# Products of q and k computed in two halves of TensorE's columns

## The chip, the cores and the metric

The kernel runs on one core of a Trainium2 chip. A core has TensorE (matrix products, PE in the profile, PEld for its weight loads), VectorE (DVE), ScalarE (ACT), GpSimd (POOL) and the queues of SyncE (SP), each with its own list of instructions. They work side by side and wait for each other by semaphores. The metric is the device time of one execution in microseconds, the median of several runs.

## The reference

The input is one image of 384 channels and 192 x 192 pixels. Layer 0 is attention over channels, layer 1 a product with binarized weights. Cut to what matters:

```python
x = x + attention(group_norm(x))            # layer 0
x = x + binary_conv(group_norm(x))          # layer 1

def attention(x):                           # 8 heads of 48 channels each
    qkv = einsum('bchw,oc->bohw', x, w_qkv) + b_qkv        # 384 -> 1152 channels
    qkv = max over 2x2 pixels               # 192x192 -> 96x96 = 9216 pixels
    qkv = depthwise 3x3 convolution(qkv)
    q, k, v = split(qkv, 3, axis=1)
    q, k = q / norm(q), k / norm(k)         # over the pixels
    attn = einsum('bhcn,bhdn->bhcd', q, k) * temperature   # 48 x 48 a head
    out = sum of four top-k softmaxes of attn, each @ v
    return w_proj @ upsample(gelu(out)) + b_proj
```

The change concerns `attn`: for each head, 48 x 48 sums over 9216 pixels. Only the products within a head are used.

## The kernel before

The image is worked through in 24 units of 8 rows, which after pooling are 4 rows of 96 pixels (3 in the first unit, 5 in the last, because of the 3x3 convolution). A first pass computes the statistics of the group norm, a second one q and k (six maps of 128 channels each), a third one v (three maps) and the attention's output; then come the projection and layer 1. Each map of a unit is computed in three blocks, each with three matmuls into one PSUM buffer (three buffers in all), and VectorE takes the maxima out of PSUM:

```python
        for r0, nr, c0, ncol in BLOCKS:                       # 3 blocks
            ps = pqkv.tile([P, 512], F32, name="qkv")
            for t in range(CT):                               # CT = 3
                nc.tensor.matmul(
                    ps,
                    wq[:, t, m * P : (m + 1) * P],
                    x4[:, t, r0 : r0 + nr, c0 : c0 + ncol],
                    start=(t == 0),
                    stop=(t == CT - 1),
                )
            nc.vector.tensor_reduce(pl[...], ps.rearrange(...), AX.XY, ALU.max)
        # ... ScalarE adds the bias, ScalarE and VectorE do the 3x3 taps
```

For the products, pixels must lie on the partitions. VectorE transposes q and k in blocks of 32 x 32, and DMAs put the blocks in place (`room<-blocks` in the profile). Then chunks of 128 pixels are multiplied: q is the stationary operand (the weights), k the moving one. The sums stay in PSUM over all units, in three buffers `gram`, one for every 128 channels of q. A tile of 128 channels touches three or four heads, so 144 or 192 channels of k; these start at a multiple of 32 (B = 32), which makes 160, 192 and 160 columns:

```python
HD = C // HEADS                                               # 48
HEAD0 = [t * P // HD for t in range(CT)]
HEAD1 = [((t + 1) * P - 1) // HD for t in range(CT)]
D0 = [h * HD for h in HEAD0]
DN = [(h1 - h0 + 1) * HD for h0, h1 in zip(HEAD0, HEAD1)]     # 144, 192, 144
B0 = [d // B for d in D0]
BN = [-(-(d + n) // B) - b for d, n, b in zip(D0, DN, B0)]    # 5, 6, 5 blocks of 32
# ...
        def products(u):

            n, nk, q, k = of_unit(u)                          # nk chunks of pixels
            for i in range(nk):
                L = min(P, n * WP - i * P)
                for t in range(CT):
                    ins = nc.tensor.matmul(
                        gram[t][:, : BN[t] * B],
                        q[:L, t, i],
                        k[:L, B0[t] : B0[t] + BN[t], i],
                        start=u == 0 and i == 0,
                        stop=u == NU - 1 and i == nk - 1,
                    )
                    if u == NU - 1:
                        tc.keep_in_program_order(ins)

        for u in range(NU):
            # ...
            for m in range(2 * CT):                           # six maps: q, then k
                acc = tp.tile([P, (PR + 1) * WP], F32, name="dw")[:, : n * WP]
                qkv_unit(pqkv, xt, u, m, padded_qk[m], [(acc, 0, n)], None if u or m else bias)
                transposed(u, *divmod(m, CT), acc)
                # ... sums of squares on ScalarE
                if u and m == CT - 1:
                    products(u - 1)
                if m % CT == CT - 1:
                    moved(u, m // CT)                         # the DMAs of the blocks

    def gathered():                                           # in the third pass

        products(NU - 1)
        for t in range(CT):
            at = D0[t] - B0[t] * B
            nc.vector.tensor_copy(gsb[:, t, : DN[t]], gram[t][:, at : at + DN[t]])
        last_products.close()
```

The products of a unit are thus issued in the middle of the next unit. 22 units have three full chunks; the first one has a last chunk of 32 pixels, the last unit has four chunks. A scheduler orders the instructions of each engine; `keep_in_program_order` pins an instruction relative to others that are pinned.

Two other places of the kernel are used for comparison. The product of attention and v already works in four groups of 32 rows of the array, with a quarter of the channels in each:

```python
            for t in range(CT):
                for p in range(NP):                           # NP = 4
                    rows = slice(p * Q, (p + 1) * Q)          # Q = 32
                    nc.tensor.matmul(
                        pss[p][:PAIR],                        # PAIR = 96
                        aT[rows, t, p * PAIR : (p + 1) * PAIR],
                        chunk[c][rows, t, cols],              # 512 columns
                        start=(t == 0), stop=(t == CT - 1),
                    )
```

And the bias of q, k and v is corrected once, with nine matmuls that have one moving column each:

```python
        for m in range(NM):                                   # NM = 9
            nc.tensor.matmul(ps[:, m : m + 1], wg[:, m * P : (m + 1) * P], shift, start=True, stop=True)
```

Of the kernel before, what the change touches and what calls it, by code (L numbers as in the profile page):

```python
# [20 lines left out]
P = 128  # L21
C = 384
CT = C // P
# [4 lines left out]
HD = C // HEADS  # L28
# [4 lines left out]
NU = H // UR  # L33
# [9 lines left out]
HALF = P // 2  # L43
B = 32
# [27 lines left out]
D0 = [h * HD for h in HEAD0]  # L72
DN = [(h1 - h0 + 1) * HD for h0, h1 in zip(HEAD0, HEAD1)]

B0 = [d // B for d in D0]
BN = [-(-(d + n) // B) - b for d, n, b in zip(D0, DN, B0)]
PAIR = 2 * HD
NP = C // PAIR
Q = P // NP
# [27 lines left out]
def pair_rows():  # L107
# [6 lines left out]
    for p in range(NP):  # L114
        v[p * Q : (p + 1) * Q] = p * PAIR + np.stack([i, HD + i, np.where(i < HD - Q, Q + i, 2 * Q + i)], 1)
    for t in range(CT):
        o[:PAIR, t] = t * PAIR + np.arange(PAIR)
        o[PAIR:, t] = CT * PAIR + t * Q + i
    assert sorted(v.flat) == sorted(o.flat) == list(range(C))
# [28 lines left out]
def conv_preact_kernel(ctx: ExitStack, tc: tile.TileContext, a: dict, out: bass.AP):  # L148
    nc = tc.nc
# [27 lines left out]
    def unit(u, pool=big, parts=1, pieces=1):  # L177
        xt = pool.tile([P, CT, UPX], F32, name="xt", tag="big")
        n = CT // parts
        for t in range(0, CT, n):  # L180

            for j in range(0, UPX, UPX // pieces if t == CT - 1 else UPX):
                px = slice(j, j + UPX // pieces if t == CT - 1 else UPX)
                nc.sync.dma_start(xt[:, t : t + n, px], xv[u][:, t : t + n, px])  # L184
        return xt
# [27 lines left out]
    def right(name, bufs=1, stack=att):  # L213
        return stack.enter_context(tc.tile_pool(name=name, bufs=bufs, side="right"))

    ap = right("att")
    ssq = ap.tile([P, 2 * CT, NU], F32, name="ssq")
    gsb = ap.tile([P, CT, max(DN)], F32, name="gsb")
    osum = ap.tile([P, CT, NAB], F32, name="osum")
    aT = right("aT").tile([P, CT, C], F32, name="aT")  # L220

# [34 lines left out]
    with tc.tile_pool(name="p1", bufs=1, side="right") as p1, tc.tile_pool(name="p1ps", bufs=2, space=PSUM) as psp:  # L256
# [17 lines left out]
        for i in range(NU):  # L274
            u = NU - 1 - i
# [7 lines left out]
            for t in range(CT):  # L283
                if t == (u + 1) % SHARE:
                    at = NB + i // SHARE
# [8 lines left out]
                b, k = divmod(seen[t], BATCH)  # L294
                seen[t] += 1
                for j in range(UPX // 512):
                    at = (k * (UPX // 512) + j) * 6
# [41 lines left out]
    def rows(u):  # L339

        return (1 if u else 2), (PR if u < NU - 1 else PR + 1)

    def qkv_unit(pqkv, xt, u, m, pl, parts, before=None):


        x4 = xt.rearrange("p t (r w) -> p t r w", w=W)
        lo, hi = rows(u)
        for r0, nr, c0, ncol in BLOCKS:
            ps = pqkv.tile([P, 512], F32, name="qkv")
            for t in range(CT):  # L350
                nc.tensor.matmul(  # L351
                    ps,
                    wq[:, t, m * P : (m + 1) * P],
                    x4[:, t, r0 : r0 + nr, c0 : c0 + ncol],
                    start=(t == 0),
                    stop=(t == CT - 1),
                )
            nc.vector.tensor_reduce(  # L358
                pl[:, 2 + r0 // 2 : 2 + (r0 + nr) // 2, 1 + c0 // 2 : 1 + (c0 + ncol) // 2],
                ps.rearrange("p (i a j b) -> p i j a b", a=2, b=2, j=ncol // 2),  # L360
                AX.XY,
                ALU.max,
            )
        if before:
            before(pqkv.tile([P, 512], F32, name="qkv")[:, :NM])
        new = pl[:, 2 : 2 + PR, 1 : 1 + WP]
        nc.scalar.activation(new, new, AF.Identity, bias=bq[:, m : m + 1])  # L367
        for acc, r0, n in parts:
            acc2 = acc.rearrange("p (r w) -> p r w", w=WP)
            for k in range(9):  # L370
                r = lo - 1 + r0 + k // 3
                src = pl[:, r : r + n, k % 3 : k % 3 + WP]
                if k == 0:
                    nc.scalar.activation(acc2, src, AF.Identity, bias=bdw[:, m : m + 1], scale=wdw[:, m, 0:1])  # L374
                else:
                    nc.vector.scalar_tensor_tensor(acc2, src, wdw[:, m, k : k + 1], acc2, ALU.mult, ALU.add)  # L376
        if u < NU - 1:
            nc.scalar.copy(pl[:, 0:2, :], pl[:, PR : PR + 2, :])  # L378
# [4 lines left out]
    with pairs, tc.tile_pool(name="p2t", bufs=2, side="right") as tp:  # L383
        gram = [pg.tile([P, 512], F32, name=f"gram{t}") for t in range(CT)]
        qkT = room[:, : 2 * size].rearrange("p (s n) -> p s n", s=2)

        def of_unit(u):

            lo, hi = rows(u)
            n = hi - lo + 1  # L390
            nk = -(-n * WP // P)
            q, k = qkT[:, 0, : nk * C], qkT[:, 1, : nk * C]
            return (
                n,
                nk,
                q.rearrange("p (t k c) -> p t k c", t=CT, k=nk),
                k.rearrange("p (b k c) -> p b k c", k=nk, c=B),
            )

        def transposed(u, s, t, acc):  # L400
            n, nk, *_ = of_unit(u)
            to = blocks[:, s, : nk * C].rearrange("p (j t k c) -> p t k j c", j=NBP, t=CT, c=B)[:, t]
            full, more = divmod(n * WP // B, NBP)
            nc.vector.transpose(to[:, :full], acc[:, : full * P].rearrange("p (k j c) -> p k j c", j=NBP, c=B))  # L404
            if more:
                src = acc[:, full * P : n * WP].rearrange("p (j c) -> p j c", c=B)
                nc.vector.transpose(to[:, full, :more], src)

        def moved(u, s):

            n, nk, q, k = of_unit(u)
            for j in range(NBP):
                src = blocks[:, s, j * nk * CT * B : (j + 1) * nk * CT * B]
                for i in range(NBP):
                    at, to = slice(i * B, (i + 1) * B), slice(j * B, (j + 1) * B)
                    if s == 0:
                        nc.sync.dma_start(
                            q[to].rearrange("p t k (i c) -> p i (t k) c", i=NBP)[:, i],
                            src[at].rearrange("p (m c) -> p m c", c=B),
                        )  # L420
                    else:
                        nc.sync.dma_start(  # L422
                            k[to].rearrange("p (t i) k c -> p i t (k c)", i=NBP)[:, i],
                            src[at].rearrange("p (t m) -> p t m", t=CT),
                        )

        def products(u):

            n, nk, q, k = of_unit(u)
            for i in range(nk):  # L430
                L = min(P, n * WP - i * P)
                for t in range(CT):
                    ins = nc.tensor.matmul(  # L433
                        gram[t][:, : BN[t] * B],
                        q[:L, t, i],
                        k[:L, B0[t] : B0[t] + BN[t], i],
                        start=u == 0 and i == 0,
                        stop=u == NU - 1 and i == nk - 1,
                    )
                    if u == NU - 1:  # L440
                        tc.keep_in_program_order(ins)

        for u in range(NU):

            for v in range(u, u + KEEP + 1):
                if v not in kept:
                    kept[v] = unit(v % NU)
            xt = kept.pop(u)
            lo, hi = rows(u)
            n = hi - lo + 1  # L450
            for m in range(2 * CT):
# [3 lines that stand above are left out]
                sq = tp.tile([P, (PR + 1) * WP], BF16, name="sq", bufs=1)  # L455
                nc.scalar.activation(sq[:, : n * WP], acc, AF.Square, accum_out=ssq[:, m, u : u + 1])  # L456
# [3 lines that stand above are left out]
                    moved(u, m // CT)  # L460

    def gathered():

        products(NU - 1)
        for t in range(CT):
            at = D0[t] - B0[t] * B
            nc.vector.tensor_copy(gsb[:, t, : DN[t]], gram[t][:, at : at + DN[t]])
        last_products.close()

    wpr = ctx.enter_context(tc.tile_pool(name="wpr", bufs=1)).tile([P, CT, C], F32, name="wpr")  # L470
# [130 lines left out]
    with ExitStack() as vs:  # L601
# [15 lines left out]
        def attention(g):  # L617
# [4 lines left out]
            for t in range(CT):  # L622
                for p in range(NP):
                    rows = slice(p * Q, (p + 1) * Q)
                    nc.tensor.matmul(  # L625
                        pss[p][:PAIR],
                        aT[rows, t, p * PAIR : (p + 1) * PAIR],
                        chunk[c][rows, t, cols],
# [8 lines left out]
        for u in range(NU):  # L637
# [9 lines left out]
            for m in range(CT):  # L647
                parts = []
                for c in range(first // CR, last // CR + 1):
                    r0, r1 = max(first, c * CR), min(last, c * CR + CR - 1)  # L650
# [262 lines left out]
```

## Time and profile before

| what | value |
|---|---|
| time, median of 3 runs (lowest, highest) | 2239.83 us (2238.95, 2241.53) |
| span of the profiled execution | 2237.0 us |
| TensorE clock granted | 1.0 throughout |
| first pass (statistics), until TensorE's q and k products begin | 0 to 150 us |
| second pass (q, k and their products) | 150 to 1349 us |
| third pass (v, softmax, attention) | 1311 to 1958 us |
| projection and layer 1 | 1958 to 2237 us |

In the profile, L351 are the products that make q, k and v (`qkv`), L433 the products of q and k (`gram`), L625 attention times v (`ops`), L336 the correction of the bias. A group's row gives the line, the engine, the operation, what is written and read, the number of records, then the busy time in us and the mean duration in ns, and last the idle time before them and what ended it. The chain that ended last is followed from the last instruction back to what released each step; its lengths add up to the span, so a share of it is a share of the time. In it, a row is a start, a length and the work of that stretch. A busy TensorE says little by itself, since matmuls are pipelined; the distance from one start to the next says how long one really takes.

### The profile page before, as it was taken

The numbers are of one execution on the slowest core, as the hardware profiler recorded it, in microseconds if no ns is written. First come the engines' busy times: TensorE is split into PE (matmuls) and PEld (weight loads), VectorE is DVE, ScalarE is ACT, GpSimd is POOL, SyncE is SP. The second block draws the span as 40 slices with busy tenths as digits, with TensorE's granted clock in tenths as the row PEclk, the third lists the DMA queues.
The fourth block names the chain that finished last, engine by engine and source line by source line (L and its number), as shares of the span: only waits on it lengthen the run. The fifth ranks groups of instructions, "written<-read, shape, count | busy, mean of one in ns | idle before, by whom it ended". The sixth has DMA issues, their size and how long they took to land.

```text
span 2237.0 us, 19501 instructions
## 1 busy us (share of the span) xinstructions
PE 2085.8 (93%) x6135; PEld 989.3 (44%) x6135; DVE 1902.5 (85%) x3267; ACT 819.6 (37%) x1419; POOL 210.8 (9%) x329
## 2 busy tenths in 40 slices
PE   0049999999999999999999999999999999999998
PEld 0024444444444444444444444443444444455555
DVE  5668888888888888888888898987787878899998
ACT  4542222222222222222222221225333232398876
POOL 1000000000000000000000000000000000077765
PEclk9999999999999999999999999999999999999999
DMA  9962222222222222222222312105221212379997
GB/s 398 418 274 64 64 68 70 75 95 70 69 64 68 70 74 95 70 69 64 68 70 72 98 30 105 53 11 211 85 85 43 87 67 101 127 277 407 424 425 328
DMA packets 209719, 302.66 MB, mean 135 GB/s; under 512 B 162224, under 2 KB 165072, under 8 KB 209616
## 3 DMA queue, kind: packets, MB, share of 16 engines
q1 hardware_dynamic: 199296, 248.18, 31.8%
q10 hardware_dynamic: 10320, 53.25, 5.8%
q8 instruction: 48, 0.79, 0.1%
q14 instruction: 55, 0.45, 0.1%
HBM read 216.04 MB, written 56.62 MB: 122 GB/s over the span
## 4 chain that ended last, share of the span: by engine, by line
PE 81%; DVE 10%; DMA 5%; ACT 1%; SPq 1%; issue 0%; DVEq 0%; ACTq 0%
PE qkv L351 64%; PE l1ps L792 6%; PE yps L580 6%; DVE chunk L376 5%; DMA xt<-in_x_dram 5%; PE gram L433 3%; DVE pooled L358 2%; PE ops L625 2%; DVE dw L376 1%; SPq L184 1%; DVE xt L592 1%; ACT chunk L374 0%; PE qkv L270 0%; ACT pooled L367 0%; SPq L422 0%
## 5 line engine op out<-in xcount | busy, mean ns | idle before, releaser
L351 PE MATMUL qkv<-xt,wq 128*128 128x512 f32 x3888 | 1679.2, 593 | 0.0
L351 PEld LDWEIGHTS qkv<-xt,wq 128*128 128x128 f32 x3888 | 735.1, 190 | 918.1 <-issue 821.9
L376 DVE SCALAR_TENSOR_TENSOR dw<-pooled,small,dw 128x384 f32<-128x384 f32 (+2 forms) x1152 | 708.7, 615 | 118.8 <-ACT dw L374 93.7
L358 DVE TENSOR_REDUCE pooled<-qkv 128x128 f32<-128x512 f32 x648 | 442.5, 684 | 67.1 <-PE qkv L351 66.8
L376 DVE SCALAR_TENSOR_TENSOR chunk<-pooled,small,chunk 128x384 f32<-128x384 f32 (+3 forms) x696 | 369.5, 545 | 70.9 <-ACT chunk L374 53.7
L378 ACT COPY pooled<-pooled 128x196 f32<-128x196 f32 x207 | 73.6, 356 | 761.5 <-DVE dw L376 542.8
L367 ACT ACTIVATE pooled<-pooled,small 128x384 f32<-128x384 f32 x216 | 133.0, 616 | 402.8 <-DVE pooled L358 389.4
L773 ACT ACTIVATE signs<-xt,nmean 64x1536 fp8e4<-64x1536 f32 x144 | 226.5, 1573 | 41.7 <-PE yps L580 26.0
L792 PE MATMUL l1ps<-signs,wb 128*128 128x384 fp8e4 x864 | 152.2, 326 | 0.0
L580 PE MATMUL yps<-chunk,wpr 128*128 128x384 f32 x396 | 138.2, 487 | 2.7 <-DVE xt L592 2.7
L270 PE MATMUL qkv<-wq,late 128*32 128x384 f32 x18 | 9.0, 665 | 140.3 <-ACT late L292 140.3
L801 DVE SCALAR_TENSOR_TENSOR xt<-l1ps,small,xt 128x768 f32<-128x768 f32 x144 | 138.3, 1007 | 0.0
L592 DVE SCALAR_TENSOR_TENSOR xt<-yps,small,xt 128x768 f32<-128x768 f32 x132 | 128.1, 1012 | 10.8 <-PE yps L580 4.4
L298 DVE BATCH_NORM_STATS2 room<-xt 128x6 f32<-128x512 f32 x144 | 88.1, 678 | 51.0 <-DMA xt<-in_x_dram 50.9
L609 POOL MEMSET pooled<- 128x196 f32 x3 | 0.8, 263 | 1300.6 <-DVE dw L376 1300.6
L456 ACT ACTIVATE sq<-dw 128x384 bf16<-128x384 f32 (+2 forms) x144 | 75.3, 523 | 112.4 <-DVE dw L376 112.4
L792 PEld LDWEIGHTS <-wb 128*128 128x128 fp8e4 x864 | 83.7, 97 | 72.3 <-issue 14.2
L374 ACT ACTIVATE dw<-pooled,small 128x384 f32<-128x384 f32 (+2 forms) x144 | 100.4, 697 | 2.2
L287 ACT ACTIVATE room<-xt 128x1536 bf16<-128x1536 f32 x48 | 71.2, 1483 | 66.4 <-DMA xt<-in_x_dram 65.7
L580 PEld LDWEIGHTS yps<-chunk,wpr 128*128 128x128 f32 x396 | 73.2, 190 | 44.3 <-issue 3.6
L404 DVE STREAM_TRANSPOSE blocks<-dw 128x384 f32<-128x384 f32 (+1 forms) x144 | 82.0, 569 | 3.4
L751 POOL COPY rest<-signs 9x384 int32<-9x384 int32 (+1 forms) x144 | 72.4, 503 | 64.5 <-ACT signs L773 59.0
(115 smaller groups left out, 622.1 us busy)
## 6 DMA issues: line engine op xcount, KB each, us to landing
xt<-in_x_dram SPq DMA_DIRECT2D x81, 2304.0 KB, 13.4
out_dram<-xt ACTq DMA_DIRECT2D x17, 2304.0 KB, 15.6
room<-blocks SPq DMA_DIRECT2D x736, 36.0 KB, 2.0
xt<-in_x_dram SPq DMA_DIRECT2D x26, 768.0 KB, 9.0
out_dram<-xt ACTq DMA_DIRECT2D x12, 768.0 KB, 8.7
out_dram<-xt SPq DMA_DIRECT2D x8, 768.0 KB, 3.4
wq<-in_w_qkvT_dram ACTq DMA_DIRECT2D x1, 1728.0 KB, 15.1
room<-blocks SPq DMA_DIRECT2D x32, 48.0 KB, 2.0
```

What stands on the lines that cost most here:

```text
L298: nc.vector.bn_stats(stats[b][:, t, at : at + 6], xt[:, t, j * 512 : (j + 1) * 512])
L351: nc.tensor.matmul(ps, wq[:, t, m * P : (m + 1) * P], x4[:, t, r0 : r0 + nr, c0 : c0 + ncol], start=(t == 0), stop=(t == CT - 1),)
L358: nc.vector.tensor_reduce(pl[:, 2 + r0 // 2 : 2 + (r0 + nr) // 2, 1 + c0 // 2 : 1 + (c0 + ncol) // 2], ps.rearrange("p (i a j b) -> p i j ...
L367: nc.scalar.activation(new, new, AF.Identity, bias=bq[:, m : m + 1])
L374: nc.scalar.activation(acc2, src, AF.Identity, bias=bdw[:, m : m + 1], scale=wdw[:, m, 0:1])
L376: nc.vector.scalar_tensor_tensor(acc2, src, wdw[:, m, k : k + 1], acc2, ALU.mult, ALU.add)
L404: nc.vector.transpose(to[:, :full], acc[:, : full * P].rearrange("p (k j c) -> p k j c", j=NBP, c=B))
L580: nc.tensor.matmul(ps, wpr[:, t, m * P : (m + 1) * P], o[:, t, :], start=(t == 0), stop=(t == CT - 1),)
L592: nc.vector.scalar_tensor_tensor(x5[:, m, r], yb, bpr[:, m : m + 1], x5[:, m, r], ALU.add, ALU.add)
L773: nc.scalar.activation(rows_of(sg, p, SAT[t] - HSHIFT[t][h]), xt[p, t, :].rearrange("p (r w) -> p r w", w=W), AF.Sign, bias=nmean1[p, t : ...
L792: nc.tensor.matmul(ps[:, j, : 2 * W], wb[:, t, m * P : (m + 1) * P], rows_of(sg, slice(0, P), SAT[t])[:, r0 + 2 * j : r0 + 2 * j + 2], sta ...
L801: nc.vector.scalar_tensor_tensor(blk, ps[:, :, : 2 * W], bl1[:, m : m + 1], blk, ALU.add, ALU.add)
```

## The change

The array of TensorE has 128 columns, one for each of the stationary operand's. [...] The change splits each tile of 128 channels of q into two halves. A half of 64 channels touches only two heads, so it needs only 96 channels of k (96 or 128 columns, since they begin at a multiple of 32), where the whole tile needed 160 or 192. The purpose is that fewer columns are multiplied for nothing, with two halves at work side by side.

`SIDES` has, for each of the six halves, the first channel of k and their number: (0, 96), (48, 96), (96, 96), (192, 96), (240, 96), (288, 96). All products are pinned, and so is the first matmul of the fourth map (m == CT): the products of a unit stand in one piece ahead of it, and the array is parted once a unit. What lies outside the two heads of a half isn't computed any more, so `gsb` is zeroed at the start, and the copies out of PSUM are six rather than three.

```diff
+SIDES = [(c // HD * HD, ((c + HALF - 1) // HD - c // HD + 1) * HD) for c in range(0, C, HALF)]
@@
     gsb = ap.tile([P, CT, max(DN)], F32, name="gsb")
+    nc.gpsimd.memset(gsb, 0.0)
@@ in qkv_unit
-                nc.tensor.matmul(
+                ins = nc.tensor.matmul(
                     ps,
                     ...
                 )
+                if m == CT and t == r0 == c0 == 0:
+
+                    tc.keep_in_program_order(ins)
@@ in products
-                for t in range(CT):
+                for j, (d, n) in enumerate(SIDES):
+                    t, p = divmod(j * HALF, P)
+                    b0, b1 = d // B, -(-(d + n) // B)
                     ins = nc.tensor.matmul(
-                        gram[t][:, : BN[t] * B],
-                        q[:L, t, i],
-                        k[:L, B0[t] : B0[t] + BN[t], i],
+                        gram[t][p : p + HALF, (b0 - B0[t]) * B : (b1 - B0[t]) * B],
+                        q[:L, t, i, p : p + HALF],
+                        k[:L, b0:b1, i],
                         start=u == 0 and i == 0,
                         stop=u == NU - 1 and i == nk - 1,
                     )
-                    if u == NU - 1:
-                        tc.keep_in_program_order(ins)
+
+                    tc.keep_in_program_order(ins)
@@ in gathered
-        for t in range(CT):
-            at = D0[t] - B0[t] * B
-            nc.vector.tensor_copy(gsb[:, t, : DN[t]], gram[t][:, at : at + DN[t]])
+        for j, (d, n) in enumerate(SIDES):
+            t, p = divmod(j * HALF, P)
+            at = d - B0[t] * B
+            nc.vector.tensor_copy(gsb[p : p + HALF, t, d - D0[t] : d - D0[t] + n], gram[t][p : p + HALF, at : at + n])
```

The built program shows two moves besides. The three matmuls that sum b_proj by groups (32 weight columns, one moving column), which stood after the last unit's products, now stand after the first one of unit 0's. And in each unit VectorE's pooling of the fourth map's first block stands some ten instructions later in its list.

## The prediction

> **What bounds the kernel now.** I read the page from the top (busy shares, then the chain that ended last), then the chain in order of time, then windows cut at one unit's edges, and last the waits of VectorE in that stage. The page:
>
> ```profile
> PE 2085.8 (93%) x6135; PEld 989.3 (44%) x6135; DVE 1902.5 (85%) x3267; ACT 819.6 (37%) x1419; POOL 210.8 (9%) x329
> ...
> PE qkv L351 64%; PE l1ps L792 6%; PE yps L580 6%; DVE chunk L376 5%; DMA xt<-in_x_dram 5%; PE gram L433 3%; DVE pooled L358 2%; PE ops L625 2%; DVE dw L376 1%; SPq L184 1%; DVE xt L592 1%; ACT chunk L374 0%; PE qkv L270 0%; ACT pooled L367 0%; SPq L422 0%
> ```
>
> TensorE sets the end, and the products that the change rewrites (`gram`, L433) lie on that path with 3% of the span. The change has no more than that to play with. Their group among the costliest:
>
> ```profile
> L433 PE MATMUL gram<-room 128*128 128x160 f32 (+3 forms) x438 | 67.6, 308 | 1.0 <-DMA room<-blocks 1.0
> ```
>
> 438 records are 219 matmuls: each fp32 matmul appears as two passes, each with its own weight load. The chain in order of time (start, length, what, how many records):
>
> ```profile
> 158.06 2.10 PE qkv L336 x18
> 160.15 62.85 PE qkv L351 x146
> 223.01 2.80 PE gram L433 x18
> 225.81 48.26 PE qkv L351 x112
> 274.07 2.60 PE gram L433 x18
> 276.68 46.35 PE qkv L351 x108
> 323.02 2.61 PE gram L433 x18
> ...
> 1349.50 3.71 PE gram L433 x24
> ...
> 1534.39 2.76 PE ops L625 x24
> 1537.16 7.92 PE qkv L351 x18
> ```
>
> The chain stays on TensorE from unit to unit with no gap: 46.35 us of q and k products, 2.60 us of `gram`, and so on. So a microsecond saved in `gram` is a microsecond of the end, as long as nothing else closes in. What might is VectorE; two whole units in windows:
>
> ```profile
> core 0: us, PE busy (x) PEld busy (x) DVE busy (x) ACT busy (x) POOL busy (x), PEclk, DMA share, GB/s
> 276.68:325.63 48.95, 48.95 (x127) 23.12 (x127) 42.65 (x73) 12.95 (x30) 0.00 (x0) 1.00 0.26 73
> 325.63:374.59 48.96, 48.96 (x128) 23.13 (x127) 42.66 (x73) 12.95 (x30) 0.00 (x0) 1.00 0.26 73
> ```
>
> TensorE is busy throughout at full clock; VectorE needs 42.65 of 48.95 us and idles the other 6.3. It waits in part for ScalarE, in part for the matmuls.
>
> [...] `ops` (L625) works in four groups of 32 rows: 24 passes of 512 columns take 2.76 us, where one after another they would take 24 × 0.429 = 10.3 us. [...] nothing in this trace works in several column groups at once[...]. [...] one moving column and 128 weight columns, 2.10/18 = 117 ns a pass.
>
> **The change part by part.** Two terms first.
>
> A pass: 108 passes of 512 columns take 46.35 us, 429.2 ns each. 18 `gram` passes of (160+192+160)/3 = 170.7 columns take 2.605 us, 144.7 each. The line through both is 0.8335 ns per column plus 2.4 ns. So 96 columns cost 82.4 ns and 128 cost 109.1.
>
> A visit to another parting of the array, in and out, twice over. (a) Unit 0's `gram` ends with a chunk of 32 pixels, hence 32 rows: 2.80 us against 2.60, and the following 112 passes take 48.26 where 112 × 0.4292 = 48.07; 0.20 + 0.19 = 0.39 us. (b) `ops`: 2.76 − 6 × 0.4292 = 0.185, and 7.92 − 18 × 0.4292 = 0.195; together 0.38. [...] I take 0.34 us a visit.
>
> Removed: per chunk of 128 pixels, three matmuls of 128 weight columns against 160, 192 and 160 moving ones. Added: six of 64 weight columns against the two or three heads that each half touches: 96, 128, 96, 96, 128, 96. Even ones write partitions 0 to 63 and odd ones 64 to 127, so each half of the array's columns gets 320 moving columns a chunk. Side by side: 2 passes × (82.4 + 82.4 + 109.1) = 0.548 us a chunk[...]. Three chunks 1.643, plus the visit 0.34: 1.98 us a unit where 2.605 stand. Saved: 0.62 us.
>
> - Units 1 to 21: 21 × 0.62 = 13.0 us.
> - Unit 0: before, 2.605 + 0.39. After, 1.643 + 0.34 + 0.15 for the step to its 32-row chunk. But in the built order the three tiny matmuls that sum b_proj by group (32 weight columns) now stand after the first of its products and part the array twice more, some 0.3 + 0.3 us. Saved: 0.2 to 0.3.
> - Unit 22: 0. From about 1286.7 us the chain leaves TensorE for VectorE until unit 23's transposed blocks have landed, and the 0.99 us that TensorE waits there would only grow.
> - Unit 23: four chunks; 3.71 becomes 4 × 0.548 + 0.34 = 2.53, some 0.9 to 1.1 us saved, since VectorE waits for the matmuls after it. The b_proj sums leave this place: 0.28 us more.
>
> Moved: the pins put a unit's products ahead of the fourth map's first block, where before they stood one block (six passes) later. In the order on VectorE one pooling reduction then stands about ten instructions later in each unit. At 0.6 us apiece it comes some 2 us after its matmul is done; with three buffers of 2.57 us of matmuls each, TensorE isn't held. The three copies out of `gram` become six of half the partitions, in a place where VectorE has idle time; the memset of `gsb` lies at the start beside the loads. Both 0.
>
> Sum: 13.0 + 0.25 + 1.0 + 0.3 = 14.5 us; 2239.8 − 14.5 = 2225.3.
>
> **The rivals.**
>
> 1. *The halves overlap only in part.* If an fp32 matmul's second pass holds back the next matmul, which goes to the other half, the order is A1, A2 beside B1, B2, ...: about 0.60 us a chunk rather than 0.548. Saved 0.46 a unit; 2229. Against it: the timeline of `ops` shows four weight loads of different row groups within 0.18 us and the next four 0.43 us later, so there each first pass goes ahead of its neighbour's second.
> 2. *The halves don't overlap.* Row groups read different partitions; column halves read the same 128, two streams of fp32 at once. If reading allows one at a time, a chunk costs 12 passes over 1280 columns, 1.10 us, and a unit 3.29 + 0.34 = 3.6: 1.0 us lost. 24 times that: 2262 to 2265. For it: every fp32 pass here runs at 1.2 columns per ns (1/0.8335), so the read may be the limit. [...]
> 3. *VectorE becomes the bound.* A unit would last 48.33 us, and VectorE's work of 42.65 plus its waits for ScalarE leave a few us. It could take 1 or 2 us in all where unit 23's order on VectorE is reshuffled, not the gain.
>
> **Range and chances.** I give the first form about 55 in 100 (2222 to 2228), rival 1 about 17 (2227 to 2233), rival 2 or a mixture about 28 (2233 to 2268). Middle: 2227. Range: 2221.5 to 2254. Over 2% is 45 us either way; 68 us is all that `gram` has, and a loss would need 4.5 us a unit where 2.6 stand. So within 2% has 0.97, faster 0.01, slower 0.02.
>
> **What would show it.** `gram` in the chain near 1.8 us a unit (1.64 plus the way in), with the qkv passes after it longer by about 0.2: right. The records should start in pairs, a few ns apart, one of each half. At 2.1 rival 1 holds; at 3.3 or more rival 2. The whole unit should last 48.3 us where 48.95 stand. I am wrong in another way if a gap opens ahead of the passes after `gram`, with VectorE named as what ended it, or if the step between partings costs far more for columns than the 0.2 us that rows show.

## The result, and the profile after

| | before | changed |
|---|---|---|
| time, median | 2239.88 us (4 runs) | 2226.55 us (4 runs) |
| lowest, highest | 2238.95, 2241.53 | 2226.06, 2227.19 |
| ratio to before, 95% interval | 1 | 0.994 [0.9923, 0.9957] |

The change gains 13.3 us, 0.6%. The page of the changed kernel, engines and chain by line:

```profile
PE 2072.8 (93%) x6573; PEld 966.5 (43%) x6573; DVE 1902.6 (85%) x3270; ACT 819.6 (37%) x1419; POOL 211.3 (9%) x330
...
PE qkv L354 64%; PE l1ps L801 6%; PE yps L589 6%; DVE chunk L382 5%; DMA xt<-in_x_dram 5%; DVE pooled L364 2%; PE gram L441 2%; PE ops L634 2%; DVE dw L382 1%; SPq L186 1%; DVE xt L601 1%; ACT chunk L380 0%; ACT pooled L373 0%; PE qkv L273 0%; SPq L428 0%
```

`gram` (now L441) fell from 3 to 2% of the chain, with twice the records. Its row among the groups, and its instructions by form as the view of one tile lists them (duration in ns: least, median, most):

```profile
L441 PE MATMUL gram<-room 128*64 128x96 f32 (+1 forms) x876 | 46.0, 258 | 1.1 <-DMA room<-blocks 1.1
```

```profile
L441 PEld LDWEIGHTS gram<-room x876: 132/137/137, 221.4 to 1337.5; 128*64 128x64 f32 x176
L441 PE MATMUL gram<-room x876: 246/246/323, 221.4 to 1337.5; 128*64 128x96 f32 x117, 128*64 128x128 f32 x59
```

Twice as many records take 46.0 us where 67.6 stood. (The view names the form of 176 records of the 876.) All of them have 128 rows; there is no form with 32 rows any more, which matters below. The chain in order of time, units 0 and 1:

```profile
221.47 0.31 PE gram L441 x2
221.78 0.28 PE p3ps L206 x6
222.06 1.79 PE gram L441 x28
223.85 46.55 PE qkv L354 x108
270.40 1.80 PE gram L441 x36
272.19 46.55 PE qkv L354 x108
```

A unit's `gram` takes 1.80 us where 2.60 stood, and the 108 passes behind it 46.55 rather than 46.35: the difference is the way out of the parted array. Two whole units in windows, cut as before (columns: time, busy time of each engine and its records, clock, DMA):

```profile
273.90:322.24 48.34, 48.34 (x145) 22.11 (x144) 42.62 (x73) 12.95 (x30) 0.00 (x0) 1.00 0.27 74
322.24:370.58 48.34, 48.34 (x145) 22.11 (x144) 42.62 (x73) 12.96 (x30) 0.00 (x0) 1.00 0.27 74
```

A unit lasts 48.34 us, TensorE busy throughout. That the halves lie side by side is seen in a window of 0.03 us at the beginning of unit 1's products:

```profile
269.81 0.59 PE L354 MATMUL qkv<-xt,wq 128*128 128x512 f32 x1
270.33 0.33 PE L441 MATMUL gram<-room 128*64 128x96 f32 x2
```

Two `gram` records lie in 0.03 us, where one pass takes 0.08. They are the first passes of the two halves, 7 ns apart in the trace: with 64 stationary columns each, one writing partitions 0 to 63 of PSUM and the other 64 to 127, both are at work on the array at once.

**Where the time went**, by the distances between the same places of TensorE's list in the two profiles (the changed kernel's products stand six passes, 2.58 us, earlier; these are taken out of the second row before and of the fourth row after, so that the rows can be compared):

| stretch | before | changed | difference |
|---|---|---|---|
| start to the first q and k pass | 150.10 | 149.42 | −0.68 |
| from there to unit 1's products | 121.24 | 120.91 | −0.33 |
| 21 units up to unit 22's products | 1028.05 | 1015.21 | −12.84 |
| from there to the first attention product | 209.73 | 207.70 | −2.03 |
| from there to the first product of layer 1 | 461.21 | 464.14 | +2.93 |
| layer 1 to the last matmul | 258.13 | 258.13 | 0.00 |
| last matmul to the end | 6.02 | 7.15 | +1.13 |

The products of q and k gain 15.2 us (second to fourth row). In this profile 4.1 us are given back where the change has no line: ahead of layer 1, and behind the last matmul. The −0.68 us lie ahead of the products; over the fourteen profiles of this study that first stretch takes 149.3 to 150.4 us, split or not. The two profiled executions differ by 11.8 us, less than the medians do, because that of before is one of its fastest; the section on the pause says why.

### The profile page after: what moved, and what is told of

The parts are those of the page before. It is cut to its first block, busy times and chain, and to the rows that moved or that the text cites. A ratio compares the mean times of both kernels' runs of the same rounds, so it can differ in the third digit from the quotient of the medians.

```text
span 2225.2 us, 20427 instructions
## 1 busy us (share of the span) xinstructions
PE 2072.8 (93%) x6573; PEld 966.5 (43%) x6573; DVE 1902.6 (85%) x3270; ACT 819.6 (37%) x1419; POOL 211.3 (9%) x330
## 4 chain that ended last, share of the span: by engine, by line
PE 81%; DVE 11%; DMA 5%; ACT 1%; SPq 1%; issue 0%; DVEq 0%; ACTq 0%
PE qkv L354 64%; PE l1ps L801 6%; PE yps L589 6%; DVE chunk L382 5%; DMA xt<-in_x_dram 5%; DVE pooled L364 2%; PE gram L441 2%; PE ops L634 2%; DVE dw L382 1%; SPq L186 1%; DVE xt L601 1%; ACT chunk L380 0%; ACT pooled L373 0%; PE qkv L273 0%; SPq L428 0%
## 6 DMA issues: line engine op xcount, KB each, us to landing
xt<-in_x_dram SPq DMA_DIRECT2D x81, 2304.0 KB, 13.6
wq<-in_w_qkvT_dram ACTq DMA_DIRECT2D x1, 1728.0 KB, 15.2
```

## The experiments

Theory: the time of a unit's products is the moving columns that the busier half has to take, at 0.8335 ns plus 2.4 ns a pass, because the halves run side by side, plus one visit to the parted array. Rivals: the gain comes from the splitting itself or from the new order, and TensorE isn't the only limit. "Before" is each time the kernel before on the same chip.

| run | what | us | before | ratio, 95% interval |
|---|---|---|---|---|
| e1_turns | halves in turns | 2257.84 | 2240.16 | 1.0079 [1.0064, 1.0094] |
| e2_wide | halves, full width | 2249.29 | 2240.16 | 1.0043 [1.0026, 1.0060] |
| e3_loose | without the pins | 2237.79 | 2240.16 | 0.9989 [0.9983, 0.9996] |
| e4_pins | pins alone | 2240.10 | 2240.16 | 1.0000 [0.9992, 1.0009] |
| e5_after | changed kernel again | 2227.85 | 2240.40 | 0.9945 [0.9932, 0.9957] |
| e6_filled | with filler in the pause | 2225.43 | 2240.40 | 0.9933 [0.9921, 0.9946] |
| e7_quarters | quarters | 2223.75 | 2240.40 | 0.9925 [0.9913, 0.9938] |
| e8_quarters_filled | both | 2222.89 | 2240.40 | 0.9920 [0.9906, 0.9933] |
| e9_quarters_later | quarters, squares later | 2227.92 | 2240.39 | 0.9945 [0.9933, 0.9958] |
| e10_quarters_later_filled | and filler | 2227.19 | 2240.39 | 0.9940 [0.9926, 0.9953] |
| e11_halves_later | changed, squares later | 2227.57 | 2240.39 | 0.9944 [0.9931, 0.9956] |
| e12_before_filled | before with filler | 2238.96 | 2240.39 | 0.9994 [0.9986, 1.0002] |

### Halves in turns

```diff
-            for i in range(nk):
-                L = min(P, n * WP - i * P)
-                for j, (d, n) in enumerate(SIDES):
+            L = P
+            for i, j in [(i, j) for h in range(2) for i in range(nk) for j in range(h, len(SIDES), 2)]:
+                    d, n = SIDES[j]
```

> The same 18 half products a unit, but all nine of the lower half first, then all nine of the upper half. If TensorE issues in order and only neighbours in the list can lie side by side, the halves work in turns: 2 x 1.64 + 0.34 = 3.6 us a unit where the changed kernel has 1.98, so a unit lasts about 50.0 us and the time is near 2266 us, above both kernels. Rival: each half has a queue of its own that runs far ahead, and the order in the list doesn't matter: 48.3 us a unit, 2226.5 us.

The chain of this kernel:

```profile
422.20 3.11 PE gram L441 x34
425.31 46.55 PE qkv L354 x108
471.86 3.11 PE gram L441 x33
474.97 46.55 PE qkv L354 x108
```

The same instructions in another order cost 3.11 us rather than 1.80, a unit 49.66 rather than 48.34. So the gain needs neighbours in the list that lie side by side: in turns a unit is even longer than the 48.96 us of the kernel before. Some overlap is left all the same: 1.64 us more were expected and 1.31 came. The trace shows the upper half's first pass starting at 274.49 us, while three passes of the lower half, all ahead of it in the list, start only at 274.56, 274.64 and 274.75: the second pass of one product and both of the next. So the passes didn't start in the list's order here, and the start came ahead of what remained of two products, not of all nine.

### Halves with the whole width

```diff
-                        gram[t][p : p + HALF, (b0 - B0[t]) * B : (b1 - B0[t]) * B],
+                        gram[t][p : p + HALF, : BN[t] * B],
-                        k[:L, b0:b1, i],
+                        k[:L, B0[t] : B0[t] + BN[t], i],
```

> Halves side by side as in the changed kernel, but each half multiplies the 160, 192 and 160 columns of its whole tile. If the time is the moving columns that each half has to take, a chunk costs 2 x (135.8 + 162.4 + 135.8) = 868 ns, a unit 2.60 + 0.34 = 2.95 us, 0.96 us more than the changed kernel: about 2250 us, 10 us above the kernel before. Rival: the gain comes from the splitting itself (smaller weight loads, two streams at once), and the columns matter little: 2227 to 2232 us.

The chain:

```profile
320.35 2.76 PE gram L441 x36
323.11 46.55 PE qkv L354 x108
369.65 2.76 PE gram L441 x36
```

A unit lasts 49.30 us (369.65 − 320.35), 0.96 more than the changed kernel, as computed, and slower than the kernel before. Splitting by itself costs the visit and gains nothing; the gain is that a half needs 320 columns a chunk instead of 512.

### Without the pins, and the pins alone

```diff
e3_loose:
-                if m == CT and t == r0 == c0 == 0:
-                    tc.keep_in_program_order(ins)
...
-                    tc.keep_in_program_order(ins)
+                    if u == NU - 1:
+                        tc.keep_in_program_order(ins)
e4_pins: the kernel before, with both additions
```

> The changed kernel without its new pins. The scheduler then lets one qkv matmul in behind a unit's first half product, so the array is parted twice a unit. If a visit costs 0.34 to 0.39 us, this loses 0.35 to 0.45 us a unit: 2235 to 2237 us. Rival: the pins are worth nothing[...]: 2226 to 2228 us.

> The kernel before with the pins alone, no split: the products stand one block earlier, VectorE's order is that of the changed kernel. If the pins move nothing by themselves, 2239.9 us within 1 us. Rival: part of the gain comes from the new order: 2235 to 2238 us.

The chain of the kernel without the new pins:

```profile
420.11 0.31 PE gram L438 x2
420.42 1.06 PE qkv L354 x2
421.47 1.79 PE gram L438 x28
423.26 45.69 PE qkv L354 x106
```

One qkv matmul (two passes) has slipped in behind the first half product, and the array is parted twice a unit. A unit lasts 48.84 us, 0.50 more than with the pins; of the 13 us only 2.4 are left. The 0.50 is more than the 0.35 to 0.45 expected. The product that stands alone has no neighbour either, and its two passes of 82 ns would make up the rest (0.35 + 0.16); this sum is an estimate. The pins alone change nothing (2240.10 us; a unit 48.955 us, as before). They gain nothing of their own; they keep the price of the split at one visit a unit.

### The pause ahead of layer 1

The windows of the changed kernel's first profile, where the table above loses 2.93 us (the third number from the end is the clock):

```profile
1940.00:1944.00 4.00, 2.19 (x10) 1.04 (x8) 3.54 (x5) 2.35 (x2) 0.60 (x2) 0.94 0.00 0
1944.00:1948.00 4.00, 3.53 (x6) 2.05 (x7) 0.32 (x1) 3.94 (x3) 3.37 (x5) 0.50 0.01 2
1948.00:1952.00 4.00, 4.00 (x11) 2.13 (x10) 2.40 (x3) 3.93 (x3) 3.05 (x7) 0.70 0.00 0
```

TensorE is idle for 2.28 us there, waiting for VectorE, in both kernels. In this execution its clock was half for 6.83 us, from 1943.55 us on, which is 1.4 us after the pause began; in the profile shown of before it stayed full. In all profiles the halved stretches between the start and the last matmul are 3.41 or 6.83 us long. In the 3.41 us ahead of this one TensorE was busy for 2.05. At another place it isn't idle at all: in five profiles (e1, e3, e5, e6, e12) the clock is half for 3.41 us from about 160.1 to 160.8 us on, right behind the 18 passes of one column that correct the bias, with no gap before it; in the profile of before the same passes meet no halving. What decides whether a halved stretch comes was not shown.

What a halved stretch costs at the pause is seen in the fifth row of the table above. From the first attention product to layer 1, the six profiles with a full clock there take 461.2 us, the seven with 3.41 us at half 462.7 to 462.9, and the one with 6.83 us 464.1. These eight are all the split kernels without the filler. The filler is put into the pause, in e6 of the changed kernel and in e12 of the kernel before:

```diff
             projection(ys[1], FIRST[1], 2, range(2, CT))
+            spare = po.tile([P, ABLK], F32, name="ops")
+            for i in range(3):
+                nc.tensor.matmul(
+                    spare[:, :PPX], wpr[:, i, :P], chunk[FIRST[1] // UC][:, i, :PPX], start=(i == 0), stop=(i == CT - 1)
+                )
```

> The changed kernel again, beside the next three. In its profile the array's clock was halved for 6.8 us at 1943.6 us, after TensorE had stood still for 2.3 us, and some 3 us were lost there. [...] it returns in every run, 2226 to 2227 us; if it is chance, some runs come out 3 us faster, near 2223.5 us.

> The changed kernel with three useless projection matmuls (6 passes, about 1.95 us) put into TensorE's pause of 2.3 us ahead of layer 1. If the lost 3 us come from the clock that is halved because of this pause, the clock stays full there and the time falls to 2223 to 2224 us. Rival: the loss is of another kind, or the filler delays the work after it: 2226.5 us or more.

> The kernel before with the filler. With the clock's dips at that pause taken out of both kernels, the difference to the changed kernel with the filler (2225.4 us) should be what the products of q and k gain, 14 to 15 us by the traces: 2239.3 to 2240.3 us. Rival: the filler gains as much here as in the changed kernel, 2.4 us: 2238 us, and the halved clock explains nothing of the difference.

The windows of e6:

```profile
1942.00:1946.00 4.00, 3.83 (x15) 2.18 (x14) 3.54 (x5) 2.65 (x2) 0.89 (x2) 1.00 0.00 0
1946.00:1950.00 4.00, 3.83 (x12) 2.20 (x12) 1.64 (x3) 3.92 (x4) 3.31 (x6) 1.00 0.01 2
```

Six useless passes keep the clock at 1.00, and the kernel with more work is 2.4 us faster than the changed one (2225.43 against 2227.85). That is less than the 3 us expected, and not all of it is the pause: the two profiled executions differ by 1.6 us, of which the pause has 1.5, one stretch of 3.41 us. So a halved clock costs time at this pause. The changed kernel had such a stretch there in both of its profiles, and none of its runs was 3 us faster than the rest. The clock hardly separates the two kernels, though. The filler gains 1.4 us in the kernel before too, between the two expectations, with an interval that reaches no difference. The kernel before also has executions at a lower mean clock: of the 57 that stand beside these runs, nine have 1.000 and take 2238.8 to 2239.2 us, the others have 0.999 or 0.998 and take 2239.2 to 2241.9. The profile shown of before is one of the nine's kind (2238.8 us).

The two profiles with the filler compare the kernels at equal clock, since both have the one halved stretch near 160 us and no other. Their spans are 2238.0 and 2224.5 us, 13.6 apart (the medians 13.5). By the rows of the table: the products of q and k gain 15.2 us again (0.3 + 12.8 + 2.0), the stretch up to layer 1 is the same within 0.1 us, and the end gives back 1.6. So it is the end that takes most of what the kernel doesn't gain; the clock takes at most about a microsecond of the 12.6 to 13.3 us that lie between the medians without filler.

### Quarters

```diff
+SIDE = P // 4
-SIDES = [(c // HD * HD, ((c + HALF - 1) // HD - c // HD + 1) * HD) for c in range(0, C, HALF)]
+SIDES = [(c // HD * HD, ((c + SIDE - 1) // HD - c // HD + 1) * HD) for c in range(0, C, SIDE)]
@@ products and gathered: SIDE for HALF throughout
```

> Quarters of 32 columns rather than halves of 64: each touches one or two heads, 64 or 96 moving columns, and each of the four quarters of the array gets 64 + 96 + 64 a chunk: 2 x (55.7 + 82.4 + 55.7) = 388 ns where the halves take 548. Three chunks 1.16 us, the visit 0.31 us: 0.50 us less a unit, 23 to 24 units: 11 to 12 us less, 2214 to 2216 us. Rival: the issue of 72 small passes a unit, or four streams at once, is the limit: 2222 us or more.

> Quarters and the filler together: if both hold and the pause would have halved the clock, 2211 to 2213 us; if the pause falls well in this kernel anyway, the filler changes nothing beside the quarters alone, within 0.5 us.

TensorE, the chain's shares over three units, and the windows of two units:

```profile
414.66 1.37 PE L442 MATMUL gram<-room 128*32 128x64 f32 x72
415.96 46.94 PE L355 MATMUL qkv<-xt,wq 128*128 128x512 f32 x108
462.83 1.51 PE L442 MATMUL gram<-room 128*32 128x64 f32 x72
```

```profile
by line: DVE dw L383 55.3%; DVE pooled L365 20.1%; ACT dw L381 8.1%; ACT pooled L374 7.8%; ACT sq L465 5.8%; issue 2.1%; DVE blocks L411 1.2%
```

```profile
366.49:414.66 48.17, 48.17 (x182) 21.70 (x181) 42.53 (x73) 12.97 (x30) 0.00 (x0) 1.00 0.26 74
414.66:462.80 48.14, 48.09 (x181) 21.56 (x180) 42.51 (x73) 12.98 (x30) 0.00 (x0) 1.00 0.27 74
```

On the array the quarters do as computed: from the start of `gram` to the next qkv pass 1.30 us where nothing is waited for, 0.49 less than with halves. But the unit gets only 0.19 us shorter (48.155 on the mean of 21), and the 108 passes behind take up to 0.3 us longer. The chain has left TensorE: over three units it runs through VectorE and ScalarE alone. VectorE is busy for 42.5 of 48.2 us; of the other 5.7 some 4.3 are waits for ScalarE, which stand on that chain too. Busy for 88% was its full load. The waits show the turn (us in total, times, longest; from 300 to 1280 us, first of the changed kernel, then of the quarters):

```profile
DVE pooled L364 <- PE qkv L354: 4.1, 21, 0.4
```

```profile
PEld qkv L355 <- DVE pooled L365: 25.4, 60, 0.9
```

In the changed kernel VectorE still waits for TensorE, 0.2 us a unit, about what the quarters gained. In the quarters that wait is gone, and TensorE's weight loads wait for VectorE's pooling, which empties the PSUM buffers. The expected 11 to 12 us became 4.1. The time is what the rival said, its reason isn't: 72 passes in four groups run through in 1.30 us. Quarters with the filler make the fastest kernel of this study, 2222.89 us, 0.9 below the quarters, which is neither of the two expectations; in that profile a stretch of 3.41 us at half lies elsewhere, at 1333.65 us, where TensorE waits for the last unit's blocks.

### The squares later

```diff
                 if k == 0:
-                    nc.scalar.activation(acc2, src, AF.Identity, bias=..., scale=...)
+                    tap = nc.scalar.activation(acc2, src, AF.Identity, bias=..., scale=...)
+                    if squares:
+                        tc.keep_in_program_order(tap)
+                        squares.pop()()       # the map before: its sum of squares, pinned
```

(The values of `bias` and `scale` are left out here. Each map puts its sum of squares into `squares` instead of issuing it at once.)

> The quarters made gram 0.49 us shorter a unit, but the unit only 0.17 us, because the chain went over to VectorE and ScalarE (48.17 us a unit). In that chain a sum of squares on ScalarE (0.53 us) stands between the bias and the first tap of four maps of each unit. Here each map's sum of squares is pinned behind the next map's first tap; nothing else is changed. If that chain is the limit, it gets some 2 us shorter a unit, TensorE sets the pace again at 47.85 us, and the time falls by 22 x 0.32 = 7 us: 2216 to 2218 us. Rival: the limit lies in VectorE's own order or in the PSUM buffers: 2222 us or more.

> The same with the filler in TensorE's pause ahead of layer 1: 1 to 2 us less than without it, 2214.5 to 2217 us.

> The changed kernel with the sums of squares moved in the same way. If TensorE sets the pace of its 48.34 us a unit and the other chain ends 0.17 us below it, nothing changes in the second pass: 2227.8 us within 1.5 us (the last unit may gain a little). Rival: the changed kernel already loses time to VectorE: 2224 us or less.

My theory of that second chain fell. The quarters became slower: 2227.92 us, a unit 48.38; with the filler 2227.19, where 2214.5 to 2217 were expected. TensorE's timeline has a new gap in each unit, with VectorE as what ended it:

```profile
367.06 7.99 PE L357 MATMUL qkv<-xt,wq 128*128 128x512 f32 x18
375.34 38.89 PE L357 MATMUL qkv<-xt,wq 128*128 128x512 f32 x90 [0.29 <-DVE pooled L367]
```

The pins reordered VectorE's list as well: it now waits for ScalarE's first tap in every map (121 times between 300 and 1280 us, 97.2 us), where it did so 101 times (87.8 us). So the sum of squares wasn't the limit by itself. Which order would free that chain was not tried. With halves the same move changes nothing in the units (2227.57 us, a unit 48.343 as without it), so there the changed kernel doesn't yet lose time to that chain. Only the last unit's blocks come later: TensorE waits 1.90 us for them where it waited 0.81.

### Behind the last matmul

No run was made for the last 1.13 us; the traces bear on them. The rows of DMA issues, before and then changed (KB each, us from issue to landing):

```profile
out_dram<-xt SPq DMA_DIRECT2D x2, 384.0 KB, 3.5
```

```profile
out_dram<-xt SPq DMA_DIRECT2D x2, 384.0 KB, 4.7
```

The last two stores are issued at the same distance from the last matmul and land 1.2 us later. In the packets, the changed kernel has one of 16 KB on the queue of instructions 6.7 us ahead of the last matmul's start, which takes 1.0 us; at the end the stores' packets run 16 at a time up to 4.5 us after that start, and then one at a time for 1.1 us more. The page counts 52 packets on that queue where the kernel before had 48, and the list of TensorE is 438 records longer. Each of the ten other profiles of split kernels has such a packet in the 9 us ahead of the last matmul's start, and its stores end 5.7 to 6.2 us after that start. Before, the pins alone and the kernel before with the filler have none there, and end at 4.6. That the packet is the cause is argued from this, not tested.

## Why the prediction was right

2227.0 us predicted, 2226.55 measured. That these lie so close is luck: 2227 is a middle that the rivals' share of the chances pulled up from the mechanism's own sum of 2225.3, and no rival came. The mechanism was right and its sum 1.2 us too fast. By its steps:

- **TensorE sets the pace, `gram` lies on the path.** Held, and closer to its end than I wrote: I gave VectorE "a few us" in a unit of 48.33, and the quarters show 0.19 us (48.343 against 48.155). Rival 3 was named for small losses; it is the wall that the next step hits.
- **0.548 us a chunk, 0.34 a visit, 1.98 a unit.** 48.343 − 108 × 0.4292 = 1.99 us; less the computed 1.643 the visit is 0.35. 0.62 us saved was 0.612. The 0.34, below the 0.38 to 0.39 of the rows, was my estimate; the loads' records fit it: 190 ns with 128 columns (`gram` before) and 137 with 64 (`gram` after), 53 less. (Each half touches two heads, never three; 128 columns come from the start at a multiple of 32.) The wide halves confirm the pass model from another side, 0.96 us computed and 0.96 measured.
- **Units 1 to 21, 13.0 us.** 12.84.
- **Unit 0, 0.2 to 0.3.** 0.33, but for a wrong reason. I counted 0.15 us for a step to 32 rows. In the new loop the name `n` of SIDES hides the unit's `n`, so from the second chunk on `L` is 128: the short chunk is multiplied with all its rows, and the sums stay right because those beyond are zeros. The forms above show it. The step is saved; the b_proj sums cost some of it.
- **Unit 22 nothing; unit 23 and the b_proj sums 1.2 to 1.4.** 2.03 in all. (0.30 of it is the move of the b_proj sums: the pins alone have it too.) I had taken VectorE's chain from 1286.7 us on as rigid, and it isn't: the wait for the blocks stayed about as long (0.99 became 0.81 + 0.27 us), although TensorE came earlier.
- **Nothing else moves.** This was the mis-sized part of the sum, and it hid that unit 23 gained more than I wrote. The products gain 15.2 us where the sum had 14.5; then 1.1 us are lost at the end (1.6 at equal clock), and in the profile 2.9 at the pause. Over the runs it left 13.3.
- **Rivals 1 and 2.** Neither happened: `gram` takes 1.80 us, and at 2.1 or 3.3 they would have held. Two fp32 streams from the same 128 partitions didn't hinder each other (1.99 us a unit with the visit, 1.98 computed), nor did four (0.49 us less a unit, 0.50 computed).

## What to carry to other kernels

Splitting the array's columns paid here by the moving columns that each part no longer needs (320 columns a chunk instead of 512 for a half), not by the split itself (with all 512 the kernel took 2249.29 us, 9 more than before): compute the longest part's passes, add one visit (0.35 us), and place partners next to each other in the list (in turns a unit took 1.31 us more), with nothing of another shape between (one qkv matmul there cost 0.50 us a unit). Before the next step on the same engine, ask how far the runner-up is: VectorE, at 88% with its waits in series, had 0.19 us a unit left. What it still waited for the engine in front (0.2 us a unit) said it better than its busy share. And where a small gain is expected, look also at places that merely shift in time; of the ten profiles without the filler, eight met a halved clock at the pause, at 1.5 to 2.9 us, and two did not, so two profiles are compared at equal clock.

## What the runs showed of the hardware

- A visit to columns parted in two, in and out, cost 0.35 us; for rows it was 0.38 to 0.39.
- fp32 passes in two or four column groups ran side by side at the full 0.8335 ns per column each (a unit's products take 1.80 us in two groups and 1.30 in four, where 2.60 stood undivided).
- With nine products of one half listed ahead of nine of the other (`e1_turns`), the first pass for the free half started at 274.49 us, ahead of three passes for the busy half that stand before it in the list (274.56, 274.64 and 274.75 us).
- Around a pause of 2.28 us the clock fell to half for 3.41 or 6.83 us in eight of the ten profiles without the filler, which cost 1.5 to 1.7 or 2.9 us there; right behind 18 passes of one column it fell for 3.41 us without a pause, in five. Six useless passes in the pause kept it at 1.00 (`e6_filled`, 1942 to 1950 us).
